# A higher place in the list scheduler for the slots of a state-space recurrence (convolution, Mamba and attention hybrid)

## The chip, the cores and the metric

The kernel runs on one core of one Trainium2 chip. The time is what the device takes for one execution of the program, in microseconds; of the kernel before, three runs are given with their median. A profile of one more execution was taken by the hardware profiler. A core has five instruction queues that matter here: PE (matrix multiplication, with its weight loads shown as PEld), DVE (vector engine), ACT (scalar engine, activation functions and copies), POOL (GpSimd) and SP (which here issues nearly all DMAs).

## The reference

The input is x with 8 images of 384 channels and 32 x 32 pixels, in fp32. Layer 0 normalises x over its channels and runs a Mamba block forwards and backwards over the 1024 pixels, a 3 x 3 depthwise convolution beside it, and a residual sum. Layer 1 is causal attention with 6 heads over the 1024 pixels, and a feed-forward block whose weights are binarised in groups and whose activations are scaled by the largest absolute value; for images 5 to 7 that block returns zero. What matters for this change is the recurrence:

```
delta   = softplus(dt @ dt_proj_w + dt_proj_b)
deltaA  = exp(delta[..., None] * A)                       # 16 states for each of 384 channels
deltaBu = (delta * u)[..., None] * Bm[:, :, None, :]
h = dA * h + dBu                                          # for each of 1024 pixels, in two directions
y = einsum('bdn,bn->bd', h, c)
```

Every image has 2 directions x 384 channels x 16 states = 12288 such recurrences of 1024 steps.

## The kernel before

The recurrence of the 8 images is cut into 768 units, 96 for each image. A unit is 128 partitions (32 channels x 4 states) by 2 x 512 elements. The images come in the order 0, 1, 2, 3, 5, 6, 4, 7. The work of a unit goes over all engines:

- `s_load` (L582) and `s_row` load delta * u, delta and the rows of B and C from device memory, repeated over the partitions (SP, tiles `ud`, `dl`, `bc`);
- `s_first` (L612) multiplies `ud` by the row of B into the buffer `g` (POOL, 128 x 1024);
- `s_scan` takes exp(delta * A) into PSUM (ACT, L625, tile `da`, two banks), runs the recurrence along 512 elements with one vector instruction (DVE, L633, two per unit), keeps the last column as `carry` where the other half of the image follows (ACT, L638), and multiplies by the row of C (POOL, L639, in place in `g`);
- `s_sum` adds the states with a matmul (PE, L652, tile `y`), for two units at a time;
- `s_gate`, at the end of a group of eight units, adds the skip term and applies the gate z (DVE), and stores the result (SP).

A *slot* (`slot` inside `slots`, L1112) is the step that writes these parts for neighbouring units down together: loads for unit k + 4, the first multiplication for unit k + 2, the scan of unit k, sum and gate of unit k - 1. There are six buffers `g`, three each of `ud` and `dl`, two `da` banks and one `y` bank.

The rest of the work is cut into steps too. `before_scan` prepares an image: norm, input projection, causal convolution, SiLU, the local 3 x 3 convolution, and `delta`, whose results go to device memory, from where the slots load them. `attention` takes the gated results of the recurrence (L710 is its first matmul), then norm, query, key and value, scores (L800), exponentials (L833), transposes (L883), weighted values (L897) and projection (L950). `feed_forward` follows for five of the images (matmuls L1008 and L1052). `binarize` makes its weights once. Only image 0 is prepared ahead of all slots. The slots up to that of unit 97 are then spread among the preparation of images 1, 2 and 3 and `binarize`; later slots are spread among the attention and feed-forward of images that have been through the recurrence and the preparation of the images to come, by due times that the last lines of the kernel function work out. Attention of the last image comes after all slots.

This gives one list of instructions in the order of the source. It is not the order that the engines get. The framework's list scheduler walks along a timeline of its own and gives each engine, among the instructions that are ready there, the one with the lowest number; the number is the instruction's place in the source. Inside `with tc.high_priority(offset=n)` instructions get a number lower by n. The kernel uses that in a few places already: the second matmul of a pair (`at_once`, offset 400), the chains of SiLU, tanh and GELU, the gate's DVE operations and the copies of transposed probabilities (offset 60). `pin` keeps the instructions so marked in source order among themselves; both POOL multiplications are pinned. What the scheduler chose is fixed in the program: on the chip each engine runs its own list in that order and waits on semaphores for the others.

Of the kernel before, what the change touches and what calls it, by code (L numbers as in the profile page):

```python
# [58 lines left out]
def kernel(  # L59
# [537 lines left out]
    def s_row(u, i):  # L597

        if u.c > 0 or u.q > 0:
            return  # L600
        r = sp.tile([P, HB], F32, name=f"bc{i}_{u.name}", tag=f"bc{i}", bufs=NG)
        rows = spilled[u.b, "rows", u.d][i * NS + u.j * SUB : i * NS + (u.j + 1) * SUB, half(u.h)]
        load(r, rows.partition_broadcast(BLK))
        sst["bc", i, u.b, u.part, u.j] = r
# [507 lines left out]
    def slots(lo, hi):  # L1112
        def at(f, k):
            if 0 <= k < len(units):
                f(units[k])

        def slot(k):
            at(s_load, k + AHEAD + 2)
            at(lambda u: s_row(u, 0), k + AHEAD + 2)
            at(lambda u: s_row(u, 1), k + 2)  # L1120
            at(s_first, k + AHEAD)
            at(s_scan, k)
            at(s_sum, k - 1)
            at(s_gate, k - 1)

        return [(lambda k=k: slot(k), 5.0) for k in range(lo, hi)]

    def run(*lists):
        for f, _ in spread_over(*lists):
# [8 lines left out]

    per, ahead = len(units) // B, 3
    first = slots(-AHEAD - 2, per + 2)  # L1140
    others = slots(per + 2, len(units) + 2)

    taps = btile("taps").rearrange("p c l -> p (c l)")[:, : NC * DCONV * P]
# [99 lines left out]
```

## Time and profile before

| what | value |
|---|---|
| three runs | 4451.62, 4453.81, 4459.21 us (median 4453.81) |
| profiled execution | 4445.17 us, its span 4443.4 us |
| granted PE clock, mean | 0.869 |
| busy: PE, DVE, ACT, POOL | 3701.6, 3385.8, 2803.9, 3588.3 us |
| POOL multiplications | 2 x 768, 2370 and 2366 ns |
| DVE scans | 2 x 768, 1267 ns with a carry, 1207 ns without |
| ACT exponentials for the scans | 1536, 690 ns |
| DMA | 612.01 MB, 138 GB/s |

A row of the costliest groups names line, engine and operation, output and inputs by the program's names, shape and count; then busy microseconds and the mean nanoseconds of one, and then the idle time of that engine just before those instructions with what ended most of it. A row of waits says who waited for whom: total microseconds, times, and the longest. Numbers like L612 are lines of the kernel file.

### The profile page before, as it was taken

Reading aid. Unit: us, or ns where it says so; the run is one execution under the profiler, and the core shown is the slowest. Engines: PE = TensorE matmul, PEld = TensorE weight load, DVE = VectorE, ACT = ScalarE, POOL = GpSimd, SP = SyncE. Lnnn points to the kernel's source line nnn. Section 1 sums busy time; section 2 is a strip of 40 time slices with the busy share of each in tenths; the row PEclk is TensorE's granted clock in tenths of the full one; section 3 lists DMA queues with packets and bytes.
Section 4 is the critical chain, followed back from the end, with each engine's and each line's share of the span. In section 5 each row is a group of like instructions: output and inputs, shape, how many; then the busy total and the mean of one; then the engine's idle time right before and its main releaser. Section 6 shows DMA issues by size and latency. Waiting matters only on the chain.

```text
span 4443.4 us, 43447 instructions
## 1 busy us (share of the span) xinstructions
PE 3701.6 (83%) x12522; PEld 1421.4 (32%) x12522; DVE 3385.8 (76%) x4707; ACT 2803.9 (63%) x5383; POOL 3588.3 (81%) x1560
## 2 busy tenths in 40 slices
PE   3587786998889988889988799988999956997799
PEld 1132222333323333233332233322333312332244
DVE  6899999678977789877798867988676766667623
ACT  4767778576764767756677666776665733664334
POOL 0678889888888898799888998889989899889700
PEclk7696887989988999888998899988899877898899
DMA  6645555224363334642344623446332242224200
GB/s 214 242 150 199 189 206 205 102 98 148 123 228 116 102 126 148 208 160 100 110 137 163 212 98 109 154 148 228 103 105 95 78 146 99 95 83 146 84 18 29
DMA packets 327240, 612.01 MB, mean 138 GB/s; under 512 B 33321, under 2 KB 92121, under 8 KB 327001
## 3 DMA queue, kind: packets, MB, share of 16 engines
q1 hardware_dynamic: 317344, 593.09, 38.7%
q10 hardware_dynamic: 9656, 16.15, 1.1%
q8 instruction: 98, 1.61, 0.1%
q14 instruction: 142, 1.16, 0.1%
HBM read 443.45 MB, written 165.68 MB: 137 GB/s over the span
## 4 chain that ended last, share of the span: by engine, by line
PE 49%; DVE 27%; ACT 9%; issue 6%; POOL 5%; DMA 4%; SPq 0%; ACTq 0%; DVEq 0%; POOLq 0%
DVE g L633 13%; PE s L800 8%; PE pt L883 5%; PE qp L740 5%; PE yp L1052 5%; PE av L897 5%; PE y L652 5%; PE op L710 3%; PE in L352 2%; POOL g L612 2%; PE hp L1008 2%; POOL g L639 2%; DVE loc L411 2%; DVE u L380 2%; ACT da L625 2%
## 5 line engine op out<-in xcount | busy, mean ns | idle before, releaser
L612 POOL TENSOR_TENSOR g<-ud,bc 128x1024 f32<-128x1024 f32 x768 | 1820.1, 2370 | 401.8 <-DMA ud<-sud 145.5
L639 POOL TENSOR_TENSOR g<-g,bc 128x1024 f32<-128x1024 f32 x768 | 1816.8, 2366 | 212.8 <-ACT carry L638 113.4
L625 ACT ACTIVATE da<-dl,amat 128x512 f32<-128x512 f32 x1536 | 1054.8, 690 | 806.7 <-DVE g L633 794.1
L633 DVE TENSOR_TENSOR_SCAN g<-da,carry,g 128x512 f32<-128x512 f32 x768 | 942.8, 1267 | 216.4 <-POOL g L612 177.5
L633 DVE TENSOR_TENSOR_SCAN g<-da,g 128x512 f32<-128x512 f32 x768 | 897.9, 1207 | 154.0 <-POOL g L612 99.3
L652 PE MATMUL y<-g,gather 128*32 128x512 f32 x3072 | 470.4, 689 | 145.1 <-POOL g L639 125.3
L800 PE MATMUL s<-k,q 64*128 64x512 f32 (+3 forms) x1152 | 498.9, 618 | 67.9 <-DVE nm L813 65.4
L813 DVE CUSTOM_DVE_ANT_0 pr<-s,cmask 128x512 f32<-128x512 f32 (+3 forms) x576 | 306.2, 550 | 324.0 <-PE s L800 270.0
L1008 PE MATMUL hp<-t,w 128*128 128x512 f32 x720 | 345.7, 626 | 47.2 <-ACT h L1016 31.4
L886 ACT COPY ptn<-pt 128x512 f32<-128x512 f32 (+3 forms) x576 | 263.1, 477 | 187.2 <-PE pt L883 186.0
L1052 PE MATMUL yp<-h,w 128*128 128x512 f32 x720 | 335.5, 621 | 45.2 <-DVE h L1034 40.6
L883 PE MATMUL pt<-ident,pr 128*128 128x128 f32 x1728 | 337.4, 310 | 12.7 <-ACT ptn L886 11.3
L352 PE MATMUL in<-xn,win 128*128 128x512 f32 x576 | 290.6, 649 | 68.8 <-DVE xc L474 18.1
L883 PEld LDWEIGHTS pt<-ident,pr 128*128 128x128 f32 x1728 | 204.8, 151 | 381.2 <-ACT ptn L886 116.7
L411 DVE SCALAR_TENSOR_TENSOR loc<-xn,vec,loc 128x496 f32<-128x496 f32 (+3 forms) x384 | 265.7, 717 | 14.5 <-ACT loc L400 12.6
L833 ACT ACTIVATE pr<-pr,low 128x512 f32<-128x512 f32 (+3 forms) x384 | 241.3, 630 | 48.0 <-DVE low L827 43.7
L897 PE MATMUL av<-ptn,v 128*64 128x512 f32 (+3 forms) x1152 | 268.6, 532 | 2.2 <-ACT ptn L886 2.2
L532 PE MATMUL dp<-xd,wdt 25*128 25x512 f32 x192 | 157.6, 949 | 129.0 <-ACT du L545 105.9
L740 PE MATMUL qp<-t,wqk 128*128 128x512 f32 x576 | 253.6, 596 | 3.4 <-DVE t L313 3.4
L800 PEld LDWEIGHTS s<-k,q 64*128 64x128 f32 x1152 | 167.3, 213 | 265.2 <-DVE nm L813 160.9
L1008 PEld LDWEIGHTS hp<-t,w 128*128 128x128 f32 x720 | 137.3, 198 | 253.3 <-issue 150.9
L1052 PEld LDWEIGHTS yp<-h,w 128*128 128x128 f32 x720 | 139.3, 198 | 246.7 <-issue 181.3
(149 smaller groups left out, 4364.9 us busy)
## 6 DMA issues: line engine op xcount, KB each, us to landing
ud<-sud SPq DMA_DIRECT2D x384, 256.0 KB, 4.3
dl<-sdl SPq DMA_DIRECT2D x384, 256.0 KB, 3.3
bc<-rows SPq DMA_DIRECT2D x256, 256.0 KB, 3.8
t<-st SPq DMA_DIRECT2D x63, 512.0 KB, 6.2
su<-u SPq DMA_DIRECT2D x48, 512.0 KB, 2.9
du<-su SPq DMA_DIRECT2D x96, 256.0 KB, 4.5
sud<-du SPq DMA_DIRECT2D x96, 256.0 KB, 2.9
sdl<-du SPq DMA_DIRECT2D x96, 256.0 KB, 3.5
```

The costliest lines, as they stand in the source:

```text
L352: nc.tensor.matmul(out=mp, lhsT=st["win", c][:, k, i, :], rhs=st["xn"][:, k, half(h)], start=(k == 0), stop=(k == NC - 1),)
L612: pin(nc.gpsimd.tensor_tensor(g, ud, rows_for(u, 0), ALU.mult))
L625: nc.scalar.activation(da, sst["dl", u.b, u.c, u.part, u.q][:, i, :], AF.Exp, scale=amat[:, u.c, k, u.j : u.j + 1],)
L633: nc.vector.tensor_tensor_scan(gi[:, ::step], da[:, ::step], gi[:, ::step], first, ALU.mult, ALU.add)
L639: pin(nc.gpsimd.tensor_tensor(g, g, rows_for(u, 1), ALU.mult))
L652: mm = nc.tensor.matmul(out=y[k * BLK : (k + 1) * BLK, :], lhsT=gather, rhs=pair[k // 2][:, k % 2, :], start=(u.j == u.first_group), stop= ...
L740: nc.tensor.matmul(out=qp, lhsT=st["wqk"][:, c, o : o + P], rhs=st["xn"][:, c, half(h)], start=(c == 0), stop=(c == NC - 1),)
L800: mm = nc.tensor.matmul(out=ss[e][:, : k1 - k0], lhsT=st["q"][rows_of(e), c, chunk(qi)], rhs=st["k"][rows_of(e), c, k0:k1], start=True, st ...
L883: nc.tensor.transpose(pt[:, chunk(i)], pr[:, e, chunk(j % QT)], ident)
L897: mm = nc.tensor.matmul(out=av[rows_of(e), cols], lhsT=st["v"][:, j, hd * HD : (hd + 1) * HD], rhs=st["ptn", j, e][:, cols], start=(j == 0 ...
L1008: nc.tensor.matmul(out=hp, lhsT=st["w1"][:, c, chunk(m % 2)], rhs=st["xn"][:, c, half(h)], start=(c == 0), stop=(c == NC - 1),)
L1052: nc.tensor.matmul(out=yp, lhsT=st["w2", k // 6][:, k % 6, :], rhs=st["h", k // NC][:, k % NC, half(h)], start=(k == 0), stop=(k == NF - 1),)
```

## The change

Every slot is now written down inside a block of higher priority with an offset of 600. All its instructions, on every engine and in SP's queue, get a number lower by 600 than their place in the source; blocks of priority inside the slot count on top of that. One slot and the other work that is spread beside it take some 34 places of the source on average, so 600 places are about 18 slots. Nothing else is edited: the same instructions, buffers and data.

```diff
-        return [(lambda k=k: slot(k), 5.0) for k in range(lo, hi)]
+        def ahead_of_all(k):
+            with tc.high_priority(offset=600):
+                slot(k)
+
+        return [(lambda k=k: ahead_of_all(k), 5.0) for k in range(lo, hi)]
```

## The prediction

> **What bounds the kernel now.** I read the page first: its busy times, then its costliest groups. The PE line is 83% busy, POOL 81%, DVE 76%, so no engine fills the span.
>
> ```profile
> PE 3701.6 (83%) x12522; PEld 1421.4 (32%) x12522; DVE 3385.8 (76%) x4707; ACT 2803.9 (63%) x5383; POOL 3588.3 (81%) x1560
> ...
> L612 POOL TENSOR_TENSOR g<-ud,bc 128x1024 f32<-128x1024 f32 x768 | 1820.1, 2370 | 401.8 <-DMA ud<-sud 145.5
> L639 POOL TENSOR_TENSOR g<-g,bc 128x1024 f32<-128x1024 f32 x768 | 1816.8, 2366 | 212.8 <-ACT carry L638 113.4
> ...
> L633 DVE TENSOR_TENSOR_SCAN g<-da,carry,g 128x512 f32<-128x512 f32 x768 | 942.8, 1267 | 216.4 <-POOL g L612 177.5
> L633 DVE TENSOR_TENSOR_SCAN g<-da,g 128x512 f32<-128x512 f32 x768 | 897.9, 1207 | 154.0 <-POOL g L612 99.3
> ```
>
> To see here: POOL does nothing but two multiplications in each of 768 slots. Its first starts at 142.5 us and its last ends at 4210 us: of 4443 us, 142 go before it and 233 after it. Next, the busy times cut at every 96th second multiplication, that is by image of the recurrence (columns: length, then busy us and instructions of PE, PEld, DVE, ACT, POOL, the granted PE clock, DMA share, GB/s):
>
> ```profile
> 152.00:684.00 532.00, 399.21 (x1028) 137.71 (x1029) 487.85 (x577) 394.41 (x630) 452.13 (x192) 0.81 0.54 187
> 684.00:1194.00 510.00, 442.45 (x1536) 169.44 (x1535) 414.23 (x577) 344.12 (x680) 447.74 (x194) 0.90 0.39 133
> 1194.00:1712.00 518.00, 452.41 (x1554) 174.43 (x1553) 409.68 (x580) 343.04 (x666) 447.51 (x193) 0.89 0.42 144
> ...
> 3230.00:3607.00 377.00, 347.30 (x1467) 142.22 (x1467) 261.74 (x437) 233.37 (x556) 335.36 (x145) 0.93 0.30 102
> 3607.00:3719.00 112.00, 37.83 (x122) 8.48 (x122) 63.52 (x57) 33.40 (x50) 110.48 (x49) 0.56 0.36 121
> 3719.00:4210.00 491.00, 421.32 (x1487) 165.62 (x1487) 333.19 (x435) 260.38 (x530) 438.15 (x189) 0.88 0.29 99
> 4210.00:4443.40 233.40, 216.03 (x821) 98.40 (x817) 72.13 (x212) 96.11 (x252) 0.00 (x0) 0.95 0.08 30
> ```
>
> To see: in the first image DVE is 92% busy and POOL idles 79.9 us of 532. In slots 648 to 671 (3607 to 3719 us) nearly all other work has run out: POOL idles 1.5 us, and 24 slots take 112.1 us, 4.67 us each. That is the floor of a slot, and POOL sets it. The last wait before slot 672 is thus the recurrence's own, and the other work (attention, the next images' preparation) had ended some 100 us earlier. What other DVE work costs the slots: images 0 and 6 differ by 251 against 88 us of DVE time outside the scans (487.85 or 325.26 less 192 scans of 1.237 us) and by 79.9 against 43.1 us of idle POOL, so 0.23 us of delay per us of DVE. Last, who waits for whom:
>
> ```profile
> DVE g L633 <- POOL g L612: 276.8, 133, 5.4
> PEld y L652 <- POOL g L639: 214.2, 85, 10.7
> POOL g L612 <- DMA ud<-sud: 145.5, 10, 127.3
> POOL g L612 <- PE y L652: 145.2, 72, 7.4
> PE y L652 <- POOL g L639: 125.3, 26, 9.8
> POOL g L639 <- ACT carry L638: 113.4, 68, 11.4
> POOL g L639 <- DVE g L633: 79.8, 55, 14.5
> ```
>
> To see: POOL waits for buffers that PE has yet to read (145), for the carry on ACT (113) and for scans (80); but DVE and PE wait longer for POOL (277, and 214 + 125). Both sides are often late.
>
> **The skill.** The Trainium skill (PSUM — Partial Sum Buffer, "Engine vs sequencer instructions") says that the queues of ScalarE, VectorE and GpSimd are strictly first in, first out and that matmuls keep program order: a scan waiting for POOL holds all that stands behind it, which is what the waits above show. It (Perfetto Trace Analysis, "GPSIMD Instruction") advises timing POOL by the spacing of starts; here 4.67 us per slot against 2.370 + 2.366 by the rows: agreed. It (ScalarE: Activation LUTs, "What ACT_TABLE_LOAD costs") gives 1283 ns a load and about 2.66 us a switch; the trace has 1283 ns.
>
> **What moves.** Nothing is computed differently; I compared the instruction orders of the two built programs. POOL's order is the same. On DVE, PE and ACT the other work comes later against the slots: by 1 to 2 slots for what stood at slots 0 to 47, 7 at 48 to 95, 10 at 96 to 191, 12 to 16 from there to 671. From slot 672 on the lag is zero again, because attention of the seventh image needs slot 671's output; the last 96 slots and the tail of 233 us keep their order. So the lag is earned in the first 200 slots and given back in the stretch where little but slots was left. In instruction durations (each line's mean), DVE work outside the slots per 96 slots goes from 275, 200, 199, 195, 214, 213, 101, 104 us to 251, 192, 196, 218, 203, 212, 129, 104; before the first slot 103 to 101, in the tail 81 in both.
>
> The sum, against the profiled execution (4445.17 us, span 4443.4):
> - First image: 24 us of DVE work leave it. At 0.23 that is 5.5 us; if DVE at 92% is itself the bound, all 24. I take the middle, -15.
> - Images 1 to 5: 1021 us of DVE work before and after, so 0.
> - Image 6: 28 us more. Into a stretch with idle engines: 0; at 0.23: 6. I take +3. The cover is the hole at 3607 to 3719 us, where DVE is busy 64 and PE 38 of 112 us; without it the 28 us would cost up to 28.
> - Other DVE instructions standing between the two scans of one slot fall from about 95 to 51 in all. 44 at some 0.7 us (the L411 row has 717 ns) are 31 us taken out of chains: between 0 and 31, by the same 0.23 about 7. I take -8.
> - Head: the loads of the first two slots stand closer together in SP's queue. POOL waited 2.2 us for the second (at 147 us): -2, at worst 0.
> - Five copies that may run on either engine go from ACT to DVE (5 x 0.58 us by their row on ACT, x 0.23) and there is one table load more (1.28): together +1, between 0 and +2.
> - SP's queue: slot loads come ahead of other loads and stores. POOL waits for ud only 18 us beyond its first wait (145.5 - 127.3), so at most -18; I take 0, with the loss below.
>
> Sum: -15 + 3 - 8 - 2 + 1 = -21. That is 4424 us for a profiled execution; the median before, 4453.81, stands 8.6 above its profile, so 4433. With each term at its ends (-24, 0, -31, -2, 0, -18 and -5.5, +6, 0, 0, +2, 0): -75 to +2.5.
>
> **Rivals.** *The whole lead is kept.* At slot 672 some 16 slots are done earlier. Each was worth 4.67 us, 75 in all; DVE had to spend 2.47 us of scans on each meanwhile, so 35 to 75 remain: about 4399. For it: the hole exists, and POOL idles 485 us between 152 and 4210 us (4058 less its busy time there). Against it: both sides already wait for each other. *Work is only moved about.* DVE and PE have the same total, 0.23 holds everywhere, and savings are paid back: 4454. For it: images 1 to 5 have like idle times (about 55 to 70) with unlike mixes. The case that the change does not do what it says falls in here: a slot that lost no contest gains nothing from its place. *PE holds the queue (slower).* The y matmuls (L652) stand earlier in PE's order and still wait for POOL. They wait 214 + 125 + 39 us now, some 330 of it before slot 672; behind them stand the attention matmuls, in stretches where PE is 87 to 92% busy. If the waits grow by a third (110 us), the other work is late by that much, against a slack that shrinks to 8 slots (the last score matmuls of the sixth attention move from slot 636 to 652, and slot 660 begins the next), 37 us: 73 over, less the 21, about +52, 4505. It decides once the waits grow by more than 58 us.
>
> **How the numbers follow.** A measurement here tells 0.2% (9 us) from no change. Small gain, 4433 (own range 4410 to 4445): 0.45. Whole lead, about 4399: 0.12. Moved about, within 0.2%: 0.17. PE or another queue held, above 4463: 0.26. So faster 0.57, same 0.17, slower 0.26; the range, 4390 to 4500, reaches half into the second case and over most of the last.
>
> **What would show it.** Right: POOL's idle time in the first 96 slots falls from 80 to about 65; slots 648 to 671 no longer run at 112 us with an idle PE (PE busy there well over 38), and slot 672 starts some 20 us earlier; last 96 slots and tail keep 491 and 233 us. Wrong: PE's waits at y for POOL well above 380 us, or POOL's waits for y or for loads above 145 and 18; or a slot 672 that starts at 3719 us again with the hole only filled.

## The result and the profile after

The changed kernel takes 4403.62 us (median of 4 runs, 4396.65 to 4418.22), beside 4456.51 us for the kernel before, run next to it: a ratio of 0.9883, with a 95% interval of 0.986 to 0.9907. The profiled execution took 4405.27 us with a span of 4403.5 us, 40 us less than the profile before. The forecast was 4433 us: the sign is right and the time lies in the range, but the gain of 53 us is two and a half times the 21 us of the sum.

The first view is again the page's busy times and costliest groups.

```profile
PE 3709.6 (84%) x12522; PEld 1421.2 (32%) x12522; DVE 3379.8 (77%) x4712; ACT 2805.4 (64%) x5379; POOL 3591.6 (82%) x1560
...
L612 POOL TENSOR_TENSOR g<-ud,bc 128x1024 f32<-128x1024 f32 x768 | 1821.1, 2371 | 350.8 <-PE y L652 137.3
L639 POOL TENSOR_TENSOR g<-g,bc 128x1024 f32<-128x1024 f32 x768 | 1820.1, 2370 | 222.3 <-ACT carry L638 118.1
...
L633 DVE TENSOR_TENSOR_SCAN g<-da,carry,g 128x512 f32<-128x512 f32 x768 | 942.7, 1268 | 179.8 <-POOL g L612 132.3
L633 DVE TENSOR_TENSOR_SCAN g<-da,g 128x512 f32<-128x512 f32 x768 | 896.3, 1208 | 142.9 <-POOL g L612 107.2
```

The work is the same: no busy time moved by more than about 8 us and none of these instructions by more than 4 ns. What fell is idle time: ahead of POOL's first multiplication 401.8 became 350.8 us, and ahead of the scans 370 became 323 us. ("Idle" sums of two lines of one engine can be added, since an engine waits at one instruction at a time.)

The busy times by stretch, cut at the same slots as before (columns as in the prediction), say where:

```profile
150.00:649.00 499.00, 369.15 (x951) 120.61 (x952) 467.04 (x555) 392.08 (x625) 452.64 (x193) 0.79 0.56 193
649.00:1152.00 503.00, 445.36 (x1522) 167.98 (x1520) 404.09 (x570) 342.79 (x675) 449.24 (x193) 0.87 0.40 136
1152.00:1650.00 498.00, 431.63 (x1526) 168.04 (x1523) 401.88 (x567) 332.07 (x644) 445.55 (x192) 0.90 0.43 144
1650.00:2168.00 518.00, 452.68 (x1470) 171.61 (x1470) 422.48 (x587) 342.60 (x646) 447.81 (x194) 0.86 0.42 145
...
3178.00:3558.00 380.00, 360.60 (x1439) 143.29 (x1441) 260.15 (x461) 238.14 (x577) 334.93 (x145) 0.85 0.29 101
3558.00:3679.00 121.00, 90.93 (x414) 34.88 (x410) 83.03 (x113) 61.86 (x129) 111.86 (x50) 0.90 0.40 139
3679.00:4172.00 493.00, 418.50 (x1488) 166.27 (x1488) 332.69 (x435) 260.06 (x530) 438.01 (x189) 0.87 0.29 98
4172.00:4403.50 231.50, 213.87 (x817) 97.30 (x816) 72.14 (x212) 96.06 (x252) 0.00 (x0) 0.96 0.08 30
```

To see: the first image takes 499 us where it took 532, with 21 us less of DVE work and 30 us less of PE work inside it. The third is 20 us shorter, with 21 us less of PE work. The hole before slot 672 is filled, PE 91 us busy where it was 38, and costs 9 us more (121 for 112). Slot 672 starts 40 us earlier, and after it next to nothing changed (493 and 231.5 us for 491 and 233.4). Who waits for whom:

```profile
DVE g L633 <- POOL g L612: 239.5, 123, 5.8
PEld y L652 <- POOL g L639: 147.7, 79, 9.5
POOL g L612 <- PE y L652: 137.3, 75, 6.8
POOL g L612 <- DMA ud<-sud: 134.3, 8, 127.7
POOL g L639 <- ACT carry L638: 118.1, 69, 11.6
PE y L652 <- POOL g L639: 76.8, 15, 8.6
POOL g L639 <- DVE g L633: 74.2, 57, 10.0
...
PEld y L652 <- POOL g L612: 38.1, 46, 1.5
```

The last of these rows in the kernel before:

```profile
PEld y L652 <- POOL g L612: 39.0, 45, 3.6
```

To see: PE's waits at `y` for POOL, which the slower rival wanted to see grow by a third, fell by a quarter (147.7 + 38.1 for 214.2 + 39.0 us in the weight loads' rows). The row of the matmuls themselves (125.3 us before, 76.8 after) must not be added, as the prediction did: by the traces' times all of it lies inside the weight loads' waits. POOL's waits for loads beyond its first fell from 18 us to 7 (134.3 less 127.7).

### The profile page after: what moved, and what is told of

It is laid out like the page before. It is cut to its first block, busy times and chain, and to the rows that moved or that the text cites. A ratio compares the mean times of both kernels' runs of the same rounds, so it can differ in the third digit from the quotient of the medians.

```text
span 4403.5 us, 43481 instructions
## 1 busy us (share of the span) xinstructions
PE 3709.6 (84%) x12522; PEld 1421.2 (32%) x12522; DVE 3379.8 (77%) x4712; ACT 2805.4 (64%) x5379; POOL 3591.6 (82%) x1560
## 4 chain that ended last, share of the span: by engine, by line
PE 48%; DVE 27%; ACT 8%; issue 6%; DMA 5%; POOL 5%; SPq 1%; ACTq 0%; DVEq 0%; POOLq 0%
DVE g L633 13%; PE s L800 8%; PE yp L1052 6%; PE pt L883 5%; PE qp L740 5%; PE av L897 5%; PE y L652 5%; POOL g L612 3%; DVE loc L411 3%; PE op L710 3%; DVE u L380 2%; PE in L352 2%; POOL g L639 2%; PE ap L950 2%; ACT da L625 2%
## 5 line engine op out<-in xcount | busy, mean ns | idle before, releaser
L612 POOL TENSOR_TENSOR g<-ud,bc 128x1024 f32<-128x1024 f32 x768 | 1821.1, 2371 | 350.8 <-PE y L652 137.3
L652 PE MATMUL y<-g,gather 128*32 128x512 f32 x3072 | 472.7, 692 | 81.0 <-POOL g L639 76.8
L883 PE MATMUL pt<-ident,pr 128*128 128x128 f32 x1728 | 341.1, 313 | 16.8 <-ACT ptn L886 12.9
L352 PE MATMUL in<-xn,win 128*128 128x512 f32 x576 | 281.2, 632 | 48.3 <-DVE xn L343 17.5
L411 DVE SCALAR_TENSOR_TENSOR loc<-xn,vec,loc 128x496 f32<-128x496 f32 (+3 forms) x384 | 266.0, 719 | 18.7 <-ACT loc L400 16.9
```

The costliest lines, as they stand in the source:

```text
L411: nc.vector.scalar_tensor_tensor(to, tap, vec[:, c, V_DW + k : V_DW + k + 1], to, ALU.mult, ALU.add)
L612: pin(nc.gpsimd.tensor_tensor(g, ud, rows_for(u, 0), ALU.mult))
L652: mm = nc.tensor.matmul(out=y[k * BLK : (k + 1) * BLK, :], lhsT=gather, rhs=pair[k // 2][:, k % 2, :], start=(u.j == u.first_group), stop= ...
L883: nc.tensor.transpose(pt[:, chunk(i)], pr[:, e, chunk(j % QT)], ident)
```

## The experiments

Three theories went in. *Mix:* the gain is DVE work that leaves the full first image. *Lead:* the gain is the lead itself, the slots by which the other work trails at slot 672, wherever it was earned. *Place:* the gain is the place of single instructions, above all of the `y` sums in PE's order. "Lag" below is how many slots later a piece of the other DVE work stands than in the kernel before, read from the order of the built program. In the changed kernel it is 1.5 slots at the start, 7.5 from slot 48, 10 at slot 96, 14.4 at slot 240, 16 at slot 670 and zero from 672. Where single images are compared, one profile stands behind each number. The same program, profiled twice (the change and e13), gave images that differ by up to 6 us; where several programs put the same instructions into an image, the spread is wider: 499 to 509 us in the first image (the change, e13, e3, e11, e9) and 491 to 503 in the second (the change, e13, e3, e11). A difference of less than some 12 us in one image shows little.

All experiments compute everything. `e1` to `e3` and `e11` cut the change along the slots:

```diff
-            with tc.high_priority(offset=600):
+            with tc.high_priority(offset=600) if k < 98 else nullcontext():   # e1
+            with tc.high_priority(offset=600) if k >= 98 else nullcontext():  # e2
+            with tc.high_priority(offset=600) if k < 300 else nullcontext():  # e3
+            with tc.high_priority(offset=600) if k < 480 else nullcontext():  # e11
                 slot(k)
```

**e1, only the slots up to 97.** 

> Only the slots up to that of unit 97 keep the higher place. By the built order, the other work lags by 7 slots at slots 48 to 191 as in the whole change, but the lag is handed back in loaded stretches: 2.5 slots at 240, 2.9 at 624 to 671 (16 in the whole change). Theory 1, kept lead (each slot of lag that reaches slot 648 is worth some 3 us, 53/16): about -9 us. Theory 2, the first image is relieved (slots win over DVE work where DVE is 92% busy, and this is not paid back later): the first image falls to some 500 us as in the whole change, and the total by 30 to 50 us.

Measured: 4420.4 us, 0.9921 [0.9902, 0.994], 35 us less than before. The first image is as short as with the whole change (502 us). The lag of 7 slots then falls to 2.5 by slot 240, and images 1 and 2 take 5 and 9 us more than before. Two thirds of the gain come from priority on an eighth of the slots, and stay though most of the lag is gone: that speaks against *Lead* as the only cause.

**e2, only the slots from 98 on.** 

> Only the slots from that of unit 98 on have the higher place; the first 96 slots stand as before. Lag by the built order: 0 up to slot 191, 2 to 4 up to 431, 8 at 624 to 671. Theory 1: 8 slots, about -25 us, all of it behind slot 192. Theory 2: the first image stays at 532 us and the total within 15 us of before.

Measured: 4443.85 us, 0.9973 [0.9962, 0.9985], 12 us less. The first image is untouched (535 us). Lag builds up slowly here, to 8 slots at slot 670, and brings little. With e1 it makes 47 of the 53 us.

**e3, the slots up to 299.** 

> Higher place for the slots below 300, none after. The order is that of the whole change up to there (lag 14 slots at slot 240), then the lag is handed back: 4.5 at 336, 2.1 at 432, 5.0 at 624. Theory 1: about -15 us, and slots 288 to 384 take some 30 us longer than in the whole change. Theory 2: -40 to -53 us, with no longer stretch at 288 to 384.

Measured: 4412.71 us, 0.9905 [0.9885, 0.9925], 43 us less than before. From slot 300 the lag falls from 14.4 to 4.5 slots within one image. The busy times of that image (the fourth, slots 288 to 383):

```profile
1647.00:2187.00 540.00, 471.32 (x1613) 183.23 (x1612) 429.99 (x601) 357.07 (x679) 448.99 (x194) 0.90 0.41 141
```

and what POOL's first multiplication sat idle for in it:

```profile
  PE y L652: 42.4, 12
```

It takes 540 us where the kernel before takes 507, with 23 us more of PE work and 27 us more of DVE work in it, and POOL waits 42.4 us for `y` to leave its buffers, where the changed kernel waits 18.2 us in the same slots. Ten slots of lag given back under load cost 32 us, 3.2 us each. The three images before it are as short as with the whole change (503, 494, 501 us). The bump that *Lead* expected is there, but its total (15 us less than before) isn't: 43 of the 53 us stay.

**e11, the slots up to 479.** 

> Higher place for the slots below 480. The order is that of the change up to there; then 6.5 of 14.4 slots of lag are handed back between slots 490 and 530, in the sixth image and well ahead of the hole at 648. Kept-lag theory (what is won early is a loan that costs nothing only because it is paid back in the hole): about 3 to 4 us for each slot handed back, so +20 to +26 us against the change, 4424 to 4430, and the sixth image takes 528 us or more (508 with the change). If the early gain is no loan: 4404, and 508 us.

Measured: 4410.81 us, 0.989 [0.9872, 0.9909]. The lag falls from 14.4 to 7.7 slots in the sixth image:

```profile
2650.00:3185.00 535.00, 467.40 (x1582) 182.47 (x1581) 435.60 (x597) 355.29 (x665) 448.10 (x194) 0.91 0.42 143
```

It takes 27 us more than the 508 before, for 6.7 slots: 4 us each, with 23 us more of PE work. The predicted bump is there, but the total isn't 4424 to 4430 us: it is 51 us less than before, where the change has 53 and, run again (e13), 47. So by the medians nothing was lost that can be told from noise, which speaks against *Lead* as e3 does. In this profile images 1, 3 and 7 ran 12, 10 and 11 us shorter than in the first one of the change, with the same work in them.

The next three take the change apart by instructions.

```diff
             at(s_scan, k)
-            at(s_sum, k - 1)
+            with tc.high_priority(offset=600):        # e4: all k; e5: k < 98
+                at(s_sum, k - 1)
             at(s_gate, k - 1)
```

**e4, only the sums, in all slots.** 

> Only the sums over the states (the y matmuls on PE) have the higher place; loads, scans and gates stand as before. Lag 5 to 6 slots at slots 48 to 191, 8.6 at 624 to 671. Theory 1: about -28 us. Theory 2 (DVE contests): the scans win nothing by themselves, so -10 us at most, unless the lag in the first image is what counts and not the scans, then about two thirds of its 33 us. A PE that holds its queue (my slower rival) would show here if anywhere: waits of PE at y for POOL well above the 379 us of before, and a time above 4456.

Measured: 4418.48 us, 0.9917 [0.99, 0.9935], 37 us less. The first image takes 508 us.

**e5, only the sums, up to slot 97.** 

> Of the slots up to that of unit 97, only the sums (y matmuls on PE) have the higher place. Theory 3, formed on the traces so far: in the first image POOL waits for buffers g that PE has not summed yet, because y stands behind long runs of convolution and projection matmuls in PE's order (32.7 us of idle POOL put down to PE y there before, 9.3 with the change). It expects nearly the gain of the whole first image: 502 to 510 us in it (532 before), and -22 to -35 us in all. Theory 2, DVE contests: scans keep their places, so at most -10 us.

Measured: 4458.02 us, 0.9999 [0.9989, 1.001]: no gain at all, though the first image is 23 us shorter. The first, third and fourth image:

```profile
154.00:663.00 509.00, 380.71 (x980) 127.56 (x981) 464.70 (x557) 392.34 (x627) 452.45 (x193) 0.80 0.55 189
...
1173.00:1719.00 546.00, 478.98 (x1615) 185.52 (x1614) 425.72 (x598) 352.54 (x678) 446.85 (x192) 0.89 0.41 137
1719.00:2242.00 523.00, 457.00 (x1558) 175.15 (x1556) 412.02 (x580) 339.37 (x660) 446.89 (x194) 0.87 0.40 138
```

The lag of 6 slots that the sums earned is handed back between slots 192 and 336: these two images take 28 and 15 us more than before (518 and 507), the third with 27 us more of PE work. Here the gain was lent.

**e6, everything but the sums, up to slot 97.** 

> The opposite: of the slots up to that of unit 97 everything but the sums has the higher place (loads, multiplications, exponentials, scans, gates). Theory 3: POOL's waits for y stay near 30 us in the first image, which takes 518 us or more; -15 us at most in all. Theory 2: 500 to 508 us in the first image, -25 to -35 us in all.

Measured: 4484.65 us, 1.0054 [1.0033, 1.0075]: slower. The first image gains 13 us:

```profile
150.00:670.00 520.00, 387.31 (x1009) 131.15 (x1010) 479.04 (x577) 398.91 (x637) 452.70 (x194) 0.80 0.55 189
```

Images 1 and 2 then cost 24 and 9 us more, for 2 slots of lag given back. That is far more than the price of e3. The second image:

```profile
670.00:1204.00 534.00, 463.10 (x1536) 174.28 (x1534) 418.10 (x581) 346.22 (x681) 449.13 (x193) 0.85 0.38 131
```

It holds as many matmuls as before (1536), but they were busy for 463 us instead of 442, at a granted PE clock of 0.85 instead of 0.90. So in this profile the work was slower, not more. Why the clock was lower isn't shown.

Why the sums' place matters in the first image is seen in the timeline of the kernel before around 320 us (start, length, engine, instruction, number of them; in brackets the idle time before it and who ended that):

```profile
317.59 2.84 PE L352 MATMUL in<-xn,win 128*128 128x512 f32 x6
320.27 13.88 PE L382 MATMUL u<-up,taps 128*128 128x512 f32 x32
334.08 1.92 PE L652 MATMUL y<-g,gather 128*32 128x512 f32 x16
...
335.29 2.37 POOL L612 TENSOR_TENSOR g<-ud,bc 128x1024 f32<-128x1024 f32 x1 [7.22 <-PE y L652]
```

32 convolution matmuls run for 13.88 us ahead of the sums, and POOL stands still for 7.22 us until the sums free a `g` buffer. The idle time ahead of POOL's first multiplication in the whole first image (who ended it, us, times), its two largest parts, before:

```profile
  PE y L652: 32.7, 8
  DVE loc L411: 10.3, 1
```

and with the change:

```profile
  PE y L652: 9.3, 8
  DVE g L633: 8.6, 3
```

The wait for `y` falls by 23 us; with the sums alone (e4) it is 16.8, with all but the sums (e6) 26.8 us. The local convolution (L411), 10.3 us ahead of a slot's work on DVE, is gone too. This is what the Trainium skill (PSUM — Partial Sum Buffer, "Engine vs sequencer instructions") says of matmuls keeping program order, here with its price. A seventh `g` buffer would have tested the same from the other side; it wasn't tried. Nor do e4 and e5 isolate this wait: in e5's first image DVE has 23 us less of work, too, and PE 19.

**e7 and e8, the binarisation of the weights moved** from beside the first slots into the attention of the first image, without and with the change:

```diff
-    beside += steps_of(binarize, w1, w1s, NC, FF, 2, "w1")
-    beside += steps_of(binarize, w2, w2s, NF, C, 8, "w2")
...
-        rest += steps_of(attention, b, fed) if i < B - 1 else []
+        made = steps_of(attention, b, fed) if i < B - 1 else []
+        if i == 0:
+            signs = steps_of(binarize, w1, w1s, NC, FF, 2, "w1")
+            signs += steps_of(binarize, w2, w2s, NF, C, 8, "w2")
+            made = spread_over(made[:34], signs) + made[34:]
+        rest += made
```

> No higher place at all. Binarising the feed-forward weights (some 40 us of DVE work in the first image: 11.2 + 10.1 + 10.1 + 7.8) is written down beside the first image's attention, that is in the second image's slots. It moves DVE work out of the fullest stretch without a change of priorities. If DVE time is the bound in the first image (the upper end of my sum, one for one): the first image about 492 us, -20 to -30 us in all. At 0.23 per us on both sides: the first image -9 us, the second +9, nothing in all. Theory 3 is near the second.

> The same move together with the whole change. If the two reliefs are independent and DVE is the bound in the first image: 4404 - 25 = about 4380. If the place of the sums was the point and DVE time is worth 0.23: 4404, the same as the change alone, within 10 us.

Measured: 4452.52 us, 0.9976 [0.9964, 0.9988], and 4411.05 us, 0.991 [0.9887, 0.9933]. The premise was wrong. In the built order this DVE work stood ahead of the first slot, not in the first image. So the first slot starts 26 us earlier (116.5 for 142.5 us), the first image hardly gets shorter (529 for 532), and images 1 and 2 take 20 and 24 us more in e7. The moved work lies at 589 to 898 us, in the second image but for its first pieces; the third has none of it, but DVE and PE hold 15 and 23 us more of other work there. Beside e7, the change still brings 41 us.

The work itself became dearer. Three groups of it in the kernel before, where POOL has nothing to do yet (columns of the costliest groups, with DVE alone in the first 142 us):

```profile
L260 DVE TENSOR_TENSOR sg_w<-sg_w,w 128x3070 f32<-128x3070 f32 (+3 forms) x4 | 10.1, 2537 | 0.8 <-ACT sg_w L259 0.8
L261 DVE TENSOR_TENSOR w<-w,sg_w 128x3070 f32<-128x3070 f32 (+3 forms) x4 | 10.1, 2536 | 0.0
L255 DVE TENSOR_SCALAR w<-w,mean_w 128x614 f32<-128x614 f32 (+3 forms) x20 | 7.8, 453 | 2.9 <-DMA w<-in_w 2.9
```

and in e7, beside the slots:

```profile
L255 DVE TENSOR_SCALAR w<-w,mean_w 128x614 f32<-128x614 f32 (+3 forms) x20 | 27.2, 1423 | 0.6 <-DMA w<-in_w 0.5
L260 DVE TENSOR_TENSOR sg_w<-sg_w,w 128x3070 f32<-128x3070 f32 (+3 forms) x4 | 15.9, 3968 | 0.4 <-ACT sg_w L259 0.4
L261 DVE TENSOR_TENSOR w<-w,sg_w 128x3070 f32<-128x3070 f32 (+3 forms) x4 | 13.6, 3391 | 0.0
```

The same 28 instructions take 56.7 us instead of 28.0; the next experiment shows why.

**e12, the changed kernel with the binarisation at the end of the work beside the first slots,** which puts most of it (54 of 64 us of DVE time) into the first image:

```diff
     beside += steps_of(before_scan, ORDER[1], ("s", "pt"), diags=diags)
-    beside += steps_of(binarize, w1, w1s, NC, FF, 2, "w1")
-    beside += steps_of(binarize, w2, w2s, NF, C, 8, "w2")
     for b in ORDER[2 : 1 + ahead]:
         beside += steps_of(before_scan, b, ("s", "pt"), diags=diags)
+    beside += steps_of(binarize, w1, w1s, NC, FF, 2, "w1")
+    beside += steps_of(binarize, w2, w2s, NF, C, 8, "w2")
```

> The change, and the binarising of the weights is written down behind the preparations of the second to fourth image instead of before two of them. In the built order its DVE work leaves the time before the first slot (44 us of DVE and loads that DVE waits for) and lies at slots 23 to 42. With the binarising moved to the second image the first slot started at 117.8 us instead of 142.7 (e8), but the second image gave that back (532 us). Here the first slot should start 20 to 25 us earlier, and the first image should take some 10 us longer, so 4385 to 4395; if DVE work is worth one for one where DVE is 92% busy, the first image takes 40 us longer and the total is 4404 to 4420.

Measured: 4415.66 us, 0.9893 [0.9869, 0.9917]. The first slot starts 22 us earlier, and the first image is

```profile
128.00:672.00 544.00, 372.35 (x928) 120.89 (x927) 510.61 (x586) 403.59 (x638) 467.86 (x193) 0.76 0.57 195
```

Against the changed kernel DVE is 43.6 us longer busy in it, POOL 15.2 us and PE 3.2; it takes 45 us more. That looks like one for one, but it isn't pure DVE work. The timeline of e12 in this image, POOL first, then DVE:

```profile
257.01 2.35 POOL L639 TENSOR_TENSOR g<-g,bc 128x1024 f32<-128x1024 f32 x1
259.32 5.46 POOL L612 TENSOR_TENSOR g<-ud,bc 128x1024 f32<-128x1024 f32 x1
264.74 2.35 POOL L639 TENSOR_TENSOR g<-g,bc 128x1024 f32<-128x1024 f32 x1
...
257.14 5.44 DVE L261 TENSOR_TENSOR w<-w,sg_w 128x3070 f32<-128x3070 f32 x1
```

The DVE instruction, which alone takes up to 3.35 us in the kernel before, begins just after a POOL multiplication, and takes as much longer as that one still runs (2.2 us, to 259.36). The next POOL multiplication begins at 259.32 and takes 5.46 us instead of 2.35: it ends 2.2 us after the DVE instruction does (262.58). The records overlap, but the times add up as if the two had run one after the other. The Trainium skill (SBUF — State Buffer, "Who interferes with whom") says so: a DVE instruction with two inputs in SBUF, and `tensor_scalar` in its faster mode, contend with a GpSimd instruction that reads SBUF for one shared port, "the other fully blocks". The trace agrees to within 0.2 us. Seven POOL multiplications of this image take 3.85 to 5.46 us, 17 us more than seven usual ones; that accounts for POOL's 15.2 us. So e12 gives a price for work of this kind, and no clean one for DVE work in general.

**The offset.** e9, e10, e14 and e15 change only the number, e13 is the changed kernel once more:

```diff
-            with tc.high_priority(offset=600):
+            with tc.high_priority(offset=300):   # e9;  1200: e10;  150: e14;  100: e15
```

> Half the offset for all slots. The built order has the same lag of the other work (7.4, 8.5, 9.3, 11.9, 13.6 slots in the first five pieces of 48, 15.8 at 624), but other neighbours in detail. If the lag and its time are what counts: within 10 us of the change (4404). If the gain is the luck of one order: anything between 4380 and 4450.

> Twice the offset. If 600 places (some 18 slots) were the limit of the lead, the lag would grow; by the built order it doesn't (15.9 slots at 624): the slots are already first wherever they are ready. Lag theory: within 10 us of 4404. Luck of one order: between 4380 and 4450.

> The change itself again, beside the next two on one chip. If its distance from the offsets of 300 and 1200 (ratio 0.983 against 0.988) belongs to its order: 0.988 again. If it was the runs: 0.983 to 0.985.

> A quarter of the offset for all slots. Lag by the built order: 1.4, 5.2, 5.2, 5.7, 6.4 slots in the first five pieces of 48, then 3 to 6 up to slot 671, where it ends at 6.3 with the hole before it. Lag as a loan, some 3 to 4 us a slot, 6 slots kept: -20 to -25 us, a ratio near 0.995. If more of the gain is in which instruction goes first and not in the lag: about -50, as with 600.

> A sixth of the offset. Lag 0.7, 4.0, 2.9, 2.7, 2.2 in the first pieces, 1.3 at slot 288, then growing without interruption to 10.4 at 528 and 10.5 at 624. Lag as a loan: 10 slots reach the hole, -32 to -40 us, of which less than half in the first image and the rest in the fourth to sixth. If only the first image matters: -15 us.

| offset | lag at slots 96, 288, 670 | median us | ratio, 95% |
|---|---|---|---|
| 100 (e15) | 3, 1, 10.5 | 4409.0 | 0.9878 [0.9857, 0.9899] |
| 150 (e14) | 5, 5, 6 | 4436.57 | 0.9934 [0.9913, 0.9955] |
| 300 (e9) | as 600 (15.8 at the end) | 4383.76 | 0.9826 [0.9807, 0.9846] |
| 600 (e13) | 10, 13, 16 | 4412.83 | 0.988 [0.9858, 0.9903] |
| 1200 (e10) | as 600 (15.9 at the end) | 4387.72 | 0.9827 [0.9805, 0.9849] |

An offset of 300 is the fastest version found, 78 us faster than the kernel before and 25 to 30 us faster than the change. More offset does not make more lag: 300, 600 and 1200 all end at 16 slots. The likely reason is that a slot can't be placed ahead of what it depends on, whatever its number. But at equal lag they differ by 0.5%, and e13, which gave 0.988 again, shows that this belongs to the programs. With less lag, e14 gained what *Lead* had expected (24 us for 20 to 25), e15 more (51 us for 32 to 40). By image, e9 and e13 differ most at the end. The last two stretches up to slot 767, of e9:

```profile
3182.00:3669.00 487.00, 439.79 (x1868) 176.36 (x1860) 345.22 (x586) 300.56 (x713) 445.63 (x193) 0.91 0.33 113
3669.00:4142.00 473.00, 407.77 (x1492) 162.55 (x1494) 333.34 (x435) 259.81 (x530) 437.76 (x189) 0.91 0.31 102
```

and of e13:

```profile
3175.00:3671.00 496.00, 447.52 (x1852) 177.82 (x1851) 342.84 (x574) 300.11 (x706) 446.33 (x193) 0.88 0.33 111
3671.00:4161.00 490.00, 416.08 (x1483) 165.72 (x1487) 333.15 (x435) 259.99 (x530) 438.03 (x190) 0.87 0.30 99
```

The last 96 slots hold the same work in both, yet take 473 and 490 us, with a granted PE clock of 0.91 and 0.87 and 8 us less of PE busy time. Over all profiles these slots took 473 to 496 us. In e12 they hold 42 more matmuls; over the other 16 profiles the time goes with the granted clock, from 496 us at 0.86 (e10) to 473 at 0.91, with a correlation of -0.83. What gives e9 the higher clock wasn't found.

**All versions together.** Twelve programs differ from the kernel before only in what has priority and by how much; with the change run twice these are thirteen results. Their difference in time against the lag that they still hold at slot 670 gives a straight line of -2 us and -4.0 us per slot, with a correlation of -0.81 and a scatter of 16 us about it (my least squares). e6 lies 27 us above it, e2 22 above, e1 and e3 22 and 21 below.

A rival that none of the three theories names is the PE clock that a run was granted (as a share of full speed, mean of the run). The 84 runs of the kernel before beside the experiments took 4443 to 4478 us at 0.859 to 0.870, the longer the lower: 3.0 us per 0.001, with a correlation of -0.83 (least squares again). And over the twelve programs (the change taken from e13) the gain in time goes closer with the gain in median clock than with the lag: a correlation of -0.96 with a scatter of 7 us, where the lag alone has -0.82 and 16 us. e9 was granted 0.009 more than the kernel before beside it, e13 0.0045, e1, e3 and e11 0.005 to 0.0065, e6 0.003 less. At 3.0 us per 0.001, some 14 of e13's 47 us and 27 of e9's 78 go with the clock (an estimate). With that taken off, the lag sorts the twelve with a scatter of 9 us, at 3.0 us per slot. The clock isn't the whole of the gain: the two profiles of before and the change have 0.869 and 0.867, and 40 us between them. Whether an order of instructions gets the higher clock because it is better, or is faster because it gets it, no run here shows.

The other regularity is by stretch. Over the profiles of all 17 kernels, the length of the first image follows its DVE busy time (465 to 510 us) with a slope of 1.01 and a correlation of 0.93; without e12, which reaches furthest, the slope is 1.17. The change takes PE work away together with the DVE work, so the two are hard to part: fitted jointly, a DVE microsecond counts 0.86 and a PE microsecond 0.40. Without the three programs that move the binarisation it is 0.63 and 0.54, and PE's busy time alone sorts the 14 profiles left as well (correlation 0.96) as DVE's (0.94). In the third and fourth image the length follows PE busy time instead, with slopes of 0.96 and 0.95 (correlations 0.98 and 0.93), though part of that is the speed of PE and not moved work: with the same work in it, the second image had 434 to 445 us of PE busy time and took 491 to 503. In the seventh, which has the hole in it, PE busy time ranges from 384 to 451 us and the slope is 0.04.

## Why the prediction was right and wrong

What the change does was foreseen: lag is earned early, in the full stretches, and given back in the hole before slot 672, after which nothing moves. For its size, four profiles have the same lag up to slot 287 (the change, e13, e3, e11), so images 0 to 2 can be averaged over them, image 3 over three (without e3), and later ones over the change and e13.

| stretch | forecast | change, first profile | mean of the like profiles |
|---|---|---|---|
| first image (mix, and DVE work between two scans) | -15 - 8 | -33 | -30 |
| images 1 and 2 | 0 | -26 | -31 |
| images 3 to 5 | 0 | +10 | +6 |
| image 6, with the hole | +3 | +12 | +9 |
| start, last 96 slots, tail | -2 | -2 | -2 |

The last column adds up to -48, the medians of the two sets of runs give -53 and -47. (The forecast's terms of +1, and of 0 for SP's queue, can't be seen in the noise.)

**The step that failed most is the zero for images 1 to 5: only DVE was priced, and five images were netted.** Of the 27 us between -21 and -48, 7 lie in the first image and 31 in images 1 and 2; images 3 to 6 take 12 back (the rest is the term of +1). The sum kept images 1 to 5 at zero because their DVE work added up to the same 1021 us. But two of them become shorter and later ones longer. And PE is the full engine there (88%), and its work moved as well: in the four like profiles images 1 and 2 hold 3048 matmuls where they held 3090, and 874 us of PE busy time where they had 895. By their share the matmuls that left account for some 12 of these 21 us (an estimate); the rest is the same work done faster. DVE was busy 17 us less in these two images. How the 31 us divide between the two engines and the clock stays open.

**The second failure is the rate of 0.23 us of delay per us of DVE work**, in the sum's first, third and fourth terms. It was worked out by comparing image 0 with image 6. These are stretches with different full engines, and the seventh holds a hole in which work is nearly free, so the quotient is a slope between two regimes and no marginal price in either. Over the programs the first image's length follows DVE's busy time by about one (0.86 beside PE's 0.40), which would make the 21 us of DVE work that left it worth 18 to 21 us. That is a fit and no experiment, and PE's share in it is uncertain. Here, too, the PE side was left out, 30 us less of it and the sums' place, though the prediction itself had named POOL's 145 us of waiting for PE to read its buffers: e5, which raises only the sums, makes the first image 23 us shorter. The -15 and -8 came near the -30 only because they were a compromise with "all 24".

**The cover was right.** The prediction let the work that comes late fall into the hole at nothing up to 6 us and named the hole as its cover, at "up to 28" without it. The hole took 9 to 12 us back of some 60 (the same image took 487 and 496 us in e9 and e10, which end with the same lag, for 489 before). In an image without that cover the lag handed back costs 3 to 4 us per slot (e3, e11: 32 and 27 us, both with 23 us more of PE work), though the totals of e3 and e11 show less of it.

**The rivals.** The rival that the whole lead is kept came nearer (4399 us against the measured 4404) than the forecast did, and its chance of 0.12 was too low. It had 16 slots at 2.2 to 4.7 us each; the line over thirteen results has 4.0, or 3.0 at an equal clock. What was held against it, that both sides already wait for each other, is true but no obstacle: an engine's waiting on average says little about a stretch in which one engine is over 90% busy. In its pure form it doesn't hold either: e1 keeps 3 slots and gains 35 us, e3 5 and 43, e11 8 and 51, e2 8 and 12. "Only moved about" is right for e5 alone, where lag earned under load is handed back under load. "PE holds the queue" fell: sums that come earlier in PE's order waited less for POOL, not more, most likely because POOL came earlier as well. Its size was overdrawn from the start, since the 330 us that it let grow counted the matmuls' 125 us twice. In SP's queue 12 of the "at most 18" us of waiting went where 0 was taken, and what that is worth was not tested apart, nor was the scans' place (-8).

**What stays open:** the 25 to 30 us between 0.988 and 0.983 at the same lag, of which some 14 go with the granted clock; what sets that clock from program to program; and why the totals of e1, e3 and e11 keep more than the lag they end with. They go with the order in detail, but no single wait was found that carries them.

## What to carry to other kernels

Price a moved piece of work by the stretch that it leaves and by the one that it enters, each at the rate of the engine that is full there (here about one for one, by fits), and next to nothing where no engine is full; don't take the rate from a comparison between stretches, nor net several stretches into one sum. Running the critical chain ahead of the rest takes time out of the full stretches that is owed later. Here it cost 9 to 12 us where the debt fell due in a hole and 27 to 32 us where it fell due under load, though the whole kernel didn't always lose that much. So look for the hole first, and count the work that moves on every engine, not on the busiest alone. And before programs are compared to a few tenths of a per cent, look at the clock that each run was granted.

## What was not expected of the hardware

- The same 96 slots at the end, with the same work, took 473 to 496 us in different programs, while two profiles of one program (the change and e13) gave 493 and 490. The granted PE clock ran from 0.86 to 0.91 in them, on the whole the lower the longer.
- DVE and POOL made each other wait for whole instructions where DVE reads two inputs from SBUF (5.44 and 5.46 us for 3.35 and 2.35), and `tensor_scalar` slowed beside POOL as well (1423 ns for 453): 28 such instructions cost 28.0 us of DVE time ahead of the slots, where POOL is idle, and 56.7 us beside them, and POOL loses about 17 us more in e12. This is the likely reason why an earlier start of the slots by 22 to 26 us (e7, e8, e12) brought little by itself (9 us in e7, nothing beside the change): the 142 us ahead of the slots were the free place of this work.
